# Two graph layers on one core: another order of the setup, bounds kept in half blocks, two buffers for the context products, and an earlier start of layer 1

## The chip, the cores and the metric

The kernel runs on one core of a Trainium2 chip. The metric is the device time of one execution in microseconds (us). Engines are named as in the profile: PE is TensorE (matmuls; PEld are its weight loads), DVE is VectorE, ACT is ScalarE, POOL is GpSimd, SP is the queue that issues most DMAs. POOL and ACT issue some DMAs too. Each engine runs its instructions in the order in which the program gives them.

## The reference

There are 8 batches of 2048 nodes with 256 features, and one adjacency matrix for all of them. Cut to what matters:

```python
def norm(x):      # mean and variance over the features
    return (x - mean(x)) / sqrt(var(x) + 1e-5)

# layer 0: attention in 4 heads of 64, softmax within chunks of 256 keys
h = maximum(norm(x), 0)
q, k, v = h @ Wq.T + bq, h @ Wk.T + bk, h @ Wv.T + bv      # split into heads
s = clip(q @ k_chunk.T / sqrt(64), -10, 10)               # for each of 8 chunks
s = where(adj == 0, -10, s)
ctx = sum over chunks of softmax(s within the chunk) @ v_chunk
out = norm(ctx @ Wo.T + bo + h) * gamma + beta
x = x + out

# layer 1: one head, additive attention over the neighbours
h = maximum(norm(x), 0)
g = h @ W
e = leaky_relu((g @ a1)[:, None] + (g @ a2)[None, :], slope=0.01)
att = softmax(where(adj == 0, -1e9, e))
x = x + maximum(att @ g, 0)
```

All values are float32.

## The kernel before

**Blocks and steps.** The nodes of a batch are cut into four blocks of 512 queries (`nb` 0 to 3) and eight chunks of 256 keys (`j`). Attention has 32 steps of one block and one chunk. A step makes four tiles of logits (`logits`, L490, PE into `ps_s`); `clip` (L530, DVE) clips them from below, and from above by `bounds`, an int8 tile that holds +80 where an edge is and -80 where none is; `exponentials` (L539, ACT); `add` (L545, POOL) halves the work of the sums; `values` (L506, PE into `ps_n`) and `sums` (L518, PE into `ps_t`) multiply with v and with ones; `invert` (L550, ACT) takes the reciprocal; `scale` (L560, DVE) makes the product `prod`, and `gather` (L565) is a DMA on POOL's queue that adds `prod` to the block's `ctxT` in memory. Three steps are in flight at once: `begin(f)` and `end(f)` work on steps f, f-1, f-2 and f-3, in an order written out by hand.

**One order for each engine.** The schedule is manual: what stands first in the program is issued first on its engine. Other work is hung into the steps as pieces: `at(n, ...)` puts a piece at half step n.

**Setup** (L1015 to L1087). For batch 0 the features are normed, turned (L375) and projected to q, k and v (`qk` L434, `values` L448). The adjacency is read in 32 parts of 128 rows by 1024 keys; 24 of them are treated in the setup, 8 inside batch 0's steps. `find` loads rows four parts ahead and calls `missing_of`: DVE compares with zero (L277) into a tile `z`; parts with `half` 0 are read in a permuted order, parts with `half` 1 are read straight and POOL permutes them (L281). `bound` turns z on PE (L292, into `ps_z`) and `keep_bounds` writes the int8 bounds by ACT (L303), into `bounds[0]` or `bounds[1]` on the chip, or else into a small `bound_part`, which a DMA on POOL's queue stores (L306). The bounds of the other blocks are fetched from DRAM (`fetch_bounds`, 1 MB a block, two buffers).

**Between attention and layer 1.** `Between` holds a block's residual, output projection (`output`, L692; `take`, L728), norm, and then the features of layer 1 (`stats1` to `norm1`, turned by `ends(0)`, multiplied with W by `ends(1)`, L814). The blocks are called zero, low, mid and last.

**Layer 1.** `weights` (L940, L946, DVE) makes a piece: the attention weights of four key tiles for one block, masked by `bounds1`; `products` (L963, PE) multiplies a piece with g. There are 16 pieces a batch. In the last batch there is no next batch to hide the passage between the layers; there three first pieces (`early(0)` to `early(2)`) are placed among `last`'s steps:

```python
            last.output(0)
            last.output(1)
            last.take(0)
            last.take(1)
            weights(1)
            mid.ends(0)
            mid.ends(1)
            ...
            accs[0] = one.accumulators(0)
            early(0)
            ...
            early(1)
            last.ends(0)
            last.ends(1)
            early(2)
```

Of the kernel before, what the change touches and what calls it, by code (L numbers as in the profile page):

```python
# [17 lines left out]
P = 128  # L18
# [10 lines left out]
def gnn_two_layers(  # L29
# [139 lines left out]
    def bound_tile():  # L169
        return xpool.tile([P, NT, NB], I8, tag="bound", name="bound", bufs=2)  # L170

    def fetch_bounds(nb):
        t = bound_tile()
        nc.sync.dma_start(t, bound_d[nb])
        return t

    def store_bounds(nb):
        nc.sync.dma_start(bound_d[nb], bounds[nb])
# [88 lines left out]
    def missing_of(rows, t, half):  # L267

        tag = "e" if in_setup[0] else "hn"
        z = work.tile([P, 2 if in_setup[0] else 1, HALF], BF16, tag=tag, name="z", bufs=5)  # L270
        aside = in_setup[0] and half
        apart = dict(t=TB, b=Q)
        if aside:
            src, dst = rows, z[:, 1, :]
        else:
            src, dst = in_blocks(rows), z[:, 0, :].rearrange("p (k t b) -> p k t b", **apart)
        nc.vector.tensor_scalar(  # L277
            dst, src, 0.0, 0.0, op0=ALU.is_equal, op1=ALU.add, accum_out=missing[:, t, half:half + 1],
        )
        if aside:  # L280
            nc.gpsimd.tensor_copy(z[:, 0, :].rearrange("p (k t b) -> p k t b", **apart), in_blocks(z[:, 1, :]))  # L281
        return z[:, 0, :]
# [11 lines left out]

    def keep_bounds(pt, t, half):

        nb, rows, cols = t // TB, slice(half * 8, (half + 1) * 8), slice((t % TB) * P, (t % TB + 1) * P)
        if nb in bounds:
            dst = bounds[nb][:, rows, cols]
# [3 lines left out]
        nc.scalar.activation(dst, pt, AF.Copy, scale=-2.0 * CLIP * SC, bias=CLIP * SC)  # L303
        if nb not in bounds:
            queue = nc.gpsimd if in_setup[0] else nc.scalar
            queue.dma_start(bound_d[nb][:, rows, cols], dst)  # L306
# [162 lines left out]
    class Attention:  # L469
# [55 lines left out]
        def clip(self, n, o):  # L525
            nb, j = self.STEPS[n]
            p, i = self.ORDER[o]
            if (n, p) not in self.e:
                self.e[n, p] = work.tile([P, 2 * KT, NB], F32, tag="e", name="e", bufs=5)
            nc.vector.scalar_tensor_tensor(  # L530
                self.e[n, p][:, i * KT:(i + 1) * KT, :], self.s.pop((n, o)), -CLIP * SC,
                bounds[nb][:, j * KT:(j + 1) * KT, :], op0=ALU.max, op1=ALU.min,
            )
# [19 lines left out]
        def scale(self, n, c):  # L553
# [3 lines left out]
            if j > 0 and c == 0:  # L557
                self.prod[n] = work.tile([P, 2, NB], F32, tag="prod", name="prod", bufs=1)
# [38 lines left out]
        def begin(self, f, pieces=()):  # L597
# [9 lines left out]
            if self.has(f - 1):  # L607
                self.clip(f - 1, 0)
# [270 lines left out]
    class Layer1:  # L879
# [56 lines left out]
        def weights(self, nb, j4):  # L936
            w = work.tile([P, 4, NB], F32, tag="e", name="w", bufs=5)
            for i in range(4):
# [5 lines left out]
                if i % 2:  # L944
                    two = w[:, i - 1:i + 1, :]
                    nc.vector.scalar_tensor_tensor(  # L946
                        two, bounds1[nb][:, j - 1:j + 1, :], 0.0, two, op0=ALU.is_gt, op1=ALU.mult
# [69 lines left out]
    rows = {i: load_rows(*nearest[i]) for i in range(4)}  # L1017
    proj.stats(0, range(TB))
# [4 lines left out]
    turn_weight(raws["v"], wvT)  # L1023
    proj.norm(0, 0)
# [16 lines left out]
    for nb in range(2):  # L1041
        bounds[nb] = bound_tile()
# [4 lines left out]
    for nb in range(NNB - 1):  # L1047
# [28 lines left out]
    att.early(0)  # L1076
    proj.qk(NNB - 1, 0)
# [6 lines left out]
    find(22, 23)  # L1084
    bound(22, 23)
    proj.values(NNB - 1)
    att.early(3)  # L1087
# [5 lines left out]
    def layer1_vector(i):  # L1093
# [12 lines left out]
        2: [lambda: store_bounds(0), lambda: store_bounds(1)],  # L1106
# [11 lines left out]
    for b in range(B):  # L1118
# [19 lines left out]
        def fetch(of, nb):  # L1138
            of[nb] = fetch_bounds(nb)
# [21 lines left out]
        else:  # L1161
            at(6, lambda: fetch(bounds, 1))
        at(PER + 4, lambda: fetch(bounds, 2))
        at(2 * PER + 4, lambda: fetch(bounds, 3))
        at(3 * PER + 4, lambda: fetch(bounds1, 0))
        at(STEPS2 + 2, lambda: fetch(bounds1, 1))
# [106 lines left out]
        else:  # L1273
            one.targets(0, TB)
            one.sources(0)
            mid.stats1(range(TB))
            mid.power1()
            mid.shift1()
            low.ends(1)
            low.sum1()  # L1280
            weights(0)
# [4 lines left out]
            last.output(1)  # L1286
            last.take(0)
            last.take(1)
            weights(1)
# [9 lines left out]
            accs[0] = one.accumulators(0)  # L1299
            early(0)  # L1300
# [6 lines left out]
            weights(2)  # L1307
            last.norm1(0)
# [13 lines left out]
            weights(4)  # L1322

# [3 lines left out]
        for i, (nb, j4) in enumerate(pieces1):  # L1327
            if not ahead and i < 3:
                continue
            if i + 2 < len(pieces1):  # L1330
                weights(i + 2)
            if nb not in accs:
# [12 lines left out]
            if j4 == 0 and nb > 0 and nb + 1 < NNB:  # L1345
                fetch(bounds1, nb + 1)
            if ahead and (nb, j4) == (NNB - 1, 0):
                fetch(bounds, 0)
# [55 lines left out]
```

## Time and profile before

| | us |
|---|---|
| median of 3 runs | 3546.02 (3544.25 to 3546.72) |
| the profiled execution: its own time | 3546.5 |
| its span, first to last instruction | 3544.7 |
| PE busy in the span | 3518.3 (99%) |
| DVE, ACT, POOL busy | 2637.4, 1946.3, 1808.7 |
| mean granted clock of PE | 0.999 |
| loads of bounds, 1 MB each | 62, landing in 6.0 at the median |
| gathers of `prod` into `ctxT` | 224, landing in 4.8 at the median |

Busy time is the union of an engine's instructions. A row of a timeline gives the start, the duration, the engine and line, the operation, what it writes and reads with sizes, how many were merged, and in brackets the idle time of the engine before it with what ended it. A row of waits gives the waiting operation, what it waited for, the total, how often, and the longest. Matmuls follow each other in a pipeline and their ends are modelled, so a PE that is shown busy can still be held up.

### The profile page before, as it was taken

What the parts mean: (1) busy time and instruction counts of PE and PEld (TensorE: products, weight loads), DVE (VectorE), ACT (ScalarE), POOL (GpSimd) and SP (SyncE); (2) the same over time, 40 slices, a digit from 0 to 9 for tenths busy, and PEclk for the clock granted to TensorE, in tenths of its full rate; (3) what the DMA queues carried; (4) which work ended last, traced back from release to release, by engine and by line L of the source; (5) the groups of instructions that cost most, each with busy time, mean ns of one, the idle gap of its engine ahead of it and who ended that gap; (6) DMA issues with size and microseconds to landing.
All of it is one profiled execution on the core that took longest, in us unless ns stands there. A gap on an engine that the chain in (4) does not pass through costs nothing.

```text
span 3544.7 us, 104427 instructions
## 1 busy us (share of the span) xinstructions
PE 3518.3 (99%) x46080; PEld 2185.4 (62%) x46080; DVE 2637.4 (74%) x3979; ACT 1946.3 (55%) x2961; POOL 1808.7 (51%) x1182
## 2 busy tenths in 40 slices
PE   8999999999999999999999999999999999999999
PEld 5455785557755577555875558655586555865568
DVE  7888677876778676786767867678586785857866
ACT  5777326764267632676336762367624676147750
POOL 2678016870178702786027850378404784048841
PEclk9999999999999999999999999999999999999999
DMA  7455423344234442344423444233442334124331
GB/s 235 116 111 124 98 75 86 85 116 86 86 78 91 116 92 71 86 86 121 93 66 86 97 108 93 72 80 91 120 104 55 81 88 122 57 55 91 80 81 42
DMA packets 169111, 329.74 MB, mean 93 GB/s; under 512 B 35664, under 2 KB 97360, under 8 KB 160464
## 3 DMA queue, kind: packets, MB, share of 16 engines
q1 hardware_dynamic: 127696, 203.51, 18.9%
q0 software_dynamic: 32640, 118.50, 18.0%
q8 instruction: 360, 5.90, 0.7%
q10 hardware_dynamic: 8320, 1.05, 0.2%
q14 instruction: 95, 0.78, 0.1%
HBM read 154.14 MB, written 51.43 MB: 58 GB/s over the span
## 4 chain that ended last, share of the span: by engine, by line
PE 97%; DVE 1%; DMA 1%; ACT 0%; issue 0%; POOL 0%; DVEq 0%; POOLq 0%; ACTq 0%
PE ps_s L490 25%; PE ps_n L506 25%; PE ps_s L963 13%; PE ps_t L518 7%; PE ps_n L963 6%; PE ps_t L963 6%; PE ps_t L714 2%; PE ps_t L434 2%; PE ps_n L434 2%; PE ps_s L434 2%; PE ps_t L448 2%; PE ps_n L448 2%; PE ps_t L814 2%; PE ps_n L814 2%; PE ps_n L692 0%; PE ps_t L692 0%
## 5 line engine op out<-in xcount | busy, mean ns | idle before, releaser
L530 DVE SCALAR_TENSOR_TENSOR e<-ps_s,bound 128x1024 f32<-128x1024 f32 x1024 | 1225.1, 1221 | 398.6 <-PE ps_s L490 396.4
L545 POOL TENSOR_TENSOR both<-e 128x1024 f32<-128x1024 f32 x512 | 1219.4, 2406 | 564.2 <-PE ps_t L518 353.5
L490 PE MATMUL ps_s<-q,k 64*32 64x512 f32 x16384 | 1431.7, 590 | 1.6 <-DVE e L530 1.4
L539 ACT ACTIVATE e<-e 128x1024 f32<-128x1024 f32 x1024 | 1050.2, 1050 | 475.6 <-DVE e L530 457.1
L506 PE MATMUL ps_n<-e,v 64*32 64x512 f32 x16384 | 1222.1, 590 | 3.5 <-DVE prod L560 3.5
L506 PEld LDWEIGHTS ps_n<-e,v 64*32 64x32 f32 x16384 | 462.5, 107 | 468.8 <-issue 386.2
L490 PEld LDWEIGHTS ps_s<-q,k 64*32 64x32 f32 x16384 | 460.6, 106 | 447.6 <-issue 332.8
L518 PE MATMUL ps_t<-both,ones 64*32 64x512 f32 x4096 | 536.4, 591 | 0.0
L963 PE MATMUL ps_s<-g,w 128*128 128x257 f32 x2048 | 448.4, 380 | 0.0
L963 PEld LDWEIGHTS ps_s<-g,w 128*128 128x128 f32 x2048 | 388.3, 190 | 56.0
L560 DVE TENSOR_TENSOR prod<-ps_n,rz 128x512 f32<-128x512 f32 x448 | 288.8, 687 | 150.9 <-PE ps_n L506 91.5
L986 POOL TENSOR_TENSOR x<-x,r 128x256 f32<-128x256 f32 x124 | 90.5, 744 | 459.2 <-ACT r L984 458.4
L946 DVE SCALAR_TENSOR_TENSOR w<-bound,w 128x1024 f32<-128x1024 int8 x256 | 314.7, 1229 | 8.7
L354 POOL TENSOR_TENSOR krn<-krn,mv 128x4 f32<-128x4 f32 x28 | 6.8, 242 | 570.6 <-DVE w L940 570.6
L963 PE MATMUL ps_n<-g,w 128*128 128x257 f32 x1024 | 292.4, 382 | 0.0
L963 PE MATMUL ps_t<-g,w 128*128 128x257 f32 x1024 | 289.7, 379 | 0.0
L550 ACT ACTIVATE rz<-ps_t 128x512 f32<-128x512 f32 x256 | 152.6, 596 | 222.5 <-PE ps_t L518 194.7
L940 DVE TENSOR_SCALAR w<-src,cd 128x512 f32<-128x512 f32 x512 | 263.3, 556 | 7.0 <-ACT src L921 6.6
L963 PEld LDWEIGHTS ps_n<-g,w 128*128 128x128 f32 x1024 | 192.8, 190 | 44.4 <-issue 17.6
L565 POOL DMA_DIRECT2D ctxT<-prod x224 | 191.0, 853 | 55.6 <-DVE prod L560 47.9
L963 PEld LDWEIGHTS ps_t<-g,w 128*128 128x128 f32 x1024 | 193.8, 189 | 28.1
L551 ACT ACTIVATE rz<-rz 128x512 f32<-128x512 f32 x256 | 161.4, 630 | 8.1
(137 smaller groups left out, 2908.6 us busy)
## 6 DMA issues: line engine op xcount, KB each, us to landing
ctxT<-prod POOLq DMA_DIRECT2D x224, 512.0 KB, 4.8
bound<-bound_d SPq DMA_DIRECT2D x62, 1024.0 KB, 6.0
turned_d<-squares SPq DMA_DIRECT2D x232, 128.0 KB, 2.4
hT<-turned_d SPq DMA_DIRECT2D x58, 512.0 KB, 4.4
rows<-in_adj_dram SPq DMA_DIRECT2D x32, 512.0 KB, 5.2
x<-in_x_dram SPq DMA_DIRECT2D x32, 512.0 KB, 4.7
out_dram<-x SPq DMA_DIRECT2D x31, 512.0 KB, 2.6
xp<-in_x_dram SPq DMA_DIRECT2D x28, 512.0 KB, 4.1
```

What stands on the lines that cost most here:

```text
L434: nc.tensor.matmul(in_key_order(pp) if i == 0 else pp, w[:, di, do * P:(do + 1) * P], h, start=di == 0, stop=di == FC - 1,)
L490: nc.tensor.matmul(self.s[n, o][c * Q:(c + 1) * Q, kt, :], self.k[p][rows, at:at + Q], self.q[p][rows, nb * NB:(nb + 1) * NB], start=True, ...
L506: made.append(nc.tensor.matmul(self.num[n, c][h * Q:(h + 1) * Q, :], self.v[rows, j * KT + kt, at:at + Q], self.e[n, p][rows, i * KT + kt, :],
L518: nc.tensor.matmul(self.total[n][h * Q:(h + 1) * Q, :], ones[rows, :], self.both[n, h // 2][rows, h % 2, :], start=half == 1, stop=half == 0,)
L530: nc.vector.scalar_tensor_tensor(self.e[n, p][:, i * KT:(i + 1) * KT, :], self.s.pop((n, o)), -CLIP * SC, bounds[nb][:, j * KT:(j + 1) * K ...
L539: nc.scalar.activation(e, e, AF.Exp, scale=1.0 / SC)
L545: nc.gpsimd.tensor_tensor(self.both[n, p], e[:, 0], e[:, 1], op=ALU.add)
L560: nc.vector.tensor_tensor(dst[:, c, :], self.num.pop((n, c)), self.rz[n], op=ALU.mult)
L565: nc.gpsimd.dma_start(self.ctxT[nb], self.prod.pop(n), accum_op=ALU.add)
L940: nc.vector.tensor_scalar(w[:, i, :], self.src[nb], self.cd[:, 0, j:j + 1], self.cd[:, 1, j:j + 1], op0=ALU.mult, op1=ALU.max,)
L946: nc.vector.scalar_tensor_tensor(two, bounds1[nb][:, j - 1:j + 1, :], 0.0, two, op0=ALU.is_gt, op1=ALU.mult)
L963: nc.tensor.matmul(accs[t][:, 0:F + 1], w[:, i, t * P:(t + 1) * P], g[:, j, :], start=j == 0, stop=j == NT - 1,)
```

## The change

It has six parts.

1. Setup: in every part DVE now reads the rows straight and POOL permutes (`aside` holds for both halves). Parts are turned one pair later than before, and q and k of a block stand closer together. `keep_bounds` no longer stores at once; `send_bounds` does, after the next pair of finds. Step 1's first logits and their clip come before the last block's values. 24 transposes of the identity (`warm`) are added at the start.
2. Bounds are kept, stored and fetched in halves of a block (512 KB), with three buffers for two.
3. `prod` has two buffers for one; so have the parts of bounds under two of the tags.
4. Fetches come at regular places: each eighth half step, and each second piece of layer 1.
5. In the last batch, `weights(0)` and `early(0)` come ahead of the last output projection, `weights(1)` ahead of its takes, and mid's stats behind low's end.
6. `clip` of a step's first tile is left out where it was done early.

```diff
     def bound_tile():
-        return xpool.tile([P, NT, NB], I8, tag="bound", name="bound", bufs=2)
-
-    def fetch_bounds(nb):
+        return xpool.tile([P, NT // 2, NB], I8, tag="bound", name="bound", bufs=3)
+
+    def of_half(part):
+        nb, half = part
+        return bound_d[nb][:, half * (NT // 2):(half + 1) * (NT // 2), :]
+
+    def fetch_bounds(part):
         t = bound_tile()
-        nc.sync.dma_start(t, bound_d[nb])
+        nc.sync.dma_start(t, of_half(part))
         return t
...
-        aside = in_setup[0] and half
+        aside = in_setup[0]
...
+    unsent = []
+
+    def send_bounds():
+        while unsent:
+            nb, rows, cols, dst = unsent.pop(0)
+            nc.gpsimd.dma_start(bound_d[nb][:, rows, cols], dst)
+
     def keep_bounds(pt, t, half):
...
-            dst = work.tile([P, 8, P], I8, tag=tag, name="bound_part", bufs=2 if tag == "r" else 1)
+            dst = work.tile([P, 8, P], I8, tag=tag, name="bound_part", bufs=1 if tag == "o4" else 2)
         nc.scalar.activation(dst, pt, AF.Copy, scale=-2.0 * CLIP * SC, bias=CLIP * SC)
-        if nb not in bounds:
-            queue = nc.gpsimd if in_setup[0] else nc.scalar
-            queue.dma_start(bound_d[nb][:, rows, cols], dst)
+        if (nb, half) not in bounds:
+            if in_setup[0]:
+                unsent.append((nb, rows, cols, dst))
+            else:
+                nc.scalar.dma_start(bound_d[nb][:, rows, cols], dst)
...
-                self.prod[n] = work.tile([P, 2, NB], F32, tag="prod", name="prod", bufs=1)
+                self.prod[n] = work.tile([P, 2, NB], F32, tag="prod", name="prod", bufs=2)
...
-            if self.has(f - 1):
+            if (f - 1, 0) in self.s:
                 self.clip(f - 1, 0)
...
+    def warm(times):
+        pt = ps_m()
+        for k in range(times):
+            nc.tensor.transpose(pt[:, k % TB * P:(k % TB + 1) * P], ident, ident)
+
+    warm(16)
     proj.stats(0, range(TB))
     proj.power(0)
     turn_weight(raws["q"], wqT)
     proj.shift(0)
     turn_weight(raws["k"], wkT)
     turn_weight(raws["v"], wvT)
+    warm(8)
...
     def find(*parts):
         for i in parts:
             found[i] = missing_of(rows.pop(i), *nearest[i])
+        send_bounds()
+        for i in parts:
             if i + 4 < len(nearest):
                 rows[i + 4] = load_rows(*nearest[i + 4])
...
-        find(i + 2, i + 3)
-        bound(i, i + 1)
-        proj.qk(nb, 1, ps_h)
-        find(i + 4, i + 5)
-        bound(i + 2, i + 3)
+            find(2, 3)
+            proj.qk(0, 1, ps_h)
+            bound(0, 1)
+        else:
+            bound(i - 2, i - 1)
+            find(i + 2, i + 3)
+            proj.qk(nb, 1, ps_h)
+            bound(i, i + 1)
...
         proj.turn(nb + 1, 1)
+        find(i + 4, i + 5)
...
         proj.values(nb)
+        bound(i + 2, i + 3)
         find(i + 6, i + 7)
-        bound(i + 4, i + 5)
...
     att.early(0)
+    bound(16, 17)
...
     find(22, 23)
+    att.early(3)
+    att.clip(1, 0)
     bound(22, 23)
     proj.values(NNB - 1)
-    att.early(3)
+    send_bounds()
...
+        for k in range(8):
+            at(8 * k + (40 - 24 if b == 0 and k == 3 else 12), lambda k=k: fetch(k + 3))
...
             one.targets(0, TB)
             one.sources(0)
+            weights(0)
+            low.ends(1)
+            low.sum1()
             mid.stats1(range(TB))
             mid.power1()
             mid.shift1()
-            low.ends(1)
-            low.sum1()
-            weights(0)
+            accs[0] = one.accumulators(0)
+            early(0)
             mid.norm1(0)
             mid.norm1(1)
             one.targets(TB, 2 * TB)
             last.output(0)
             last.output(1)
+            weights(1)
             last.take(0)
             last.take(1)
-            weights(1)
...
-            accs[0] = one.accumulators(0)
-            early(0)
...
             weights(2)
+            fetch(11)
...
             weights(4)
+            fetch(12)
...
+            if i % 2 == 0 and (ahead or i < 10):
+                fetch(i // 2 + 11)
```

More of the change, by code (lines that the diff above doesn't have):

```diff
@@ L169, in bound_tile, with store_bounds @@
     def bound_tile():
-        return xpool.tile([P, NT, NB], I8, tag="bound", name="bound", bufs=2)
-    def fetch_bounds(nb):
+        return xpool.tile([P, NT // 2, NB], I8, tag="bound", name="bound", bufs=3)
[3 more added lines that the diff above has]
+    def fetch_bounds(part):
         t = bound_tile()
-        nc.sync.dma_start(t, bound_d[nb])
+        nc.sync.dma_start(t, of_half(part))
         return t
-    def store_bounds(nb):
-        nc.sync.dma_start(bound_d[nb], bounds[nb])
+    def store_bounds(part):
+        nc.sync.dma_start(of_half(part), bounds[part])
     lone = const.tile([P, NT], F32, name="lone")
@@ L293, in turn_missing @@
         return pt
+    unsent = []
[3 more added lines that the diff above has]
+            nc.gpsimd.dma_start(bound_d[nb][:, rows, cols], dst)
     def keep_bounds(pt, t, half):
         nb, rows, cols = t // TB, slice(half * 8, (half + 1) * 8), slice((t % TB) * P, (t % TB + 1) * P)
-        if nb in bounds:
-            dst = bounds[nb][:, rows, cols]
+        if (nb, half) in bounds:
+            dst = bounds[nb, half][:, :, cols]
         else:
             tag = part_tags[(2 * t + half) % 4] if in_setup[0] else "r"
-            dst = work.tile([P, 8, P], I8, tag=tag, name="bound_part", bufs=2 if tag == "r" else 1)
+            dst = work.tile([P, 8, P], I8, tag=tag, name="bound_part", bufs=1 if tag == "o4" else 2)
         nc.scalar.activation(dst, pt, AF.Copy, scale=-2.0 * CLIP * SC, bias=CLIP * SC)
-        if nb not in bounds:
-            queue = nc.gpsimd if in_setup[0] else nc.scalar
-            queue.dma_start(bound_d[nb][:, rows, cols], dst)
+        if (nb, half) not in bounds:
[3 more added lines that the diff above has]
+                nc.scalar.dma_start(bound_d[nb][:, rows, cols], dst)
     def find_lone():
@@ L531, in clip @@
                 self.e[n, p][:, i * KT:(i + 1) * KT, :], self.s.pop((n, o)), -CLIP * SC,
-                bounds[nb][:, j * KT:(j + 1) * KT, :], op0=ALU.max, op1=ALU.min,
+                bounds[nb, j // 4][:, j % 4 * KT:(j % 4 + 1) * KT, :], op0=ALU.max, op1=ALU.min,
             )
@@ L946, in weights @@
                     nc.vector.scalar_tensor_tensor(
-                        two, bounds1[nb][:, j - 1:j + 1, :], 0.0, two, op0=ALU.is_gt, op1=ALU.mult
+                        two, bounds1[nb, j // 8][:, j % 8 - 1:j % 8 + 1, :], 0.0, two, op0=ALU.is_gt, op1=ALU.mult
                     )
@@ L1039, in bound @@
             keep_bounds(turn_missing(found.pop(i)), *nearest[i])
-    for nb in range(2):
-        bounds[nb] = bound_tile()
+    HALVES_OF = [(nb, half) for nb in range(NNB) for half in range(2)]
+    for part in HALVES_OF[:3]:
+        bounds[part] = bound_tile()
     proj.stats(1, range(TB))
@@ L1105, in gnn_two_layers @@
         1: [lambda: raws.update(o=load_output_weight(wo)), layer1_weight],
-        2: [lambda: store_bounds(0), lambda: store_bounds(1)],
+        2: [lambda: [store_bounds(part) for part in HALVES_OF[:3]]],
         5: [pe(lambda: turn_weight(raws["o"], woT))],
@@ L1136, in early, with fetch @@
             one.products(accs[0], ws.pop(i), i)
-        def fetch(of, nb):
-            of[nb] = fetch_bounds(nb)
+        def fetch(k):
+            of = bounds if k < 8 or k >= 16 else bounds1
+            of[HALVES_OF[k % 8]] = fetch_bounds(HALVES_OF[k % 8])
         for nb in range(NNB - 1):
@@ L1160, in gnn_two_layers @@
                 at(n + 7, lambda nb=nb: ahead.send(nb))
[L1161 to L1166, printed above, removed]
+        for k in range(8):
+            at(8 * k + (40 - 24 if b == 0 and k == 3 else 12), lambda k=k: fetch(k + 3))
         at(STEPS2 - 6, last.load)
@@ L1344, in gnn_two_layers @@
                 one.finish(nb - 1, accs[nb - 1])
[L1345 to L1348, printed above, removed]
             if j4 == 1 and nb > 0:
```

## The prediction

> **What bounds the kernel now.** I read the page first, then TensorE's waits, then the timeline round the longest of them.
>
> ```profile
> PE 3518.3 (99%) x46080; PEld 2185.4 (62%) x46080; DVE 2637.4 (74%) x3979; ACT 1946.3 (55%) x2961; POOL 1808.7 (51%) x1182
> ```
>
> TensorE is busy all the time, so only its idle time, and matmuls whose records are stretched by a wait or a slow clock, can be won. TensorE's waits:
>
> ```profile
> PE ps_z L292 <- POOL z L281: 6.8, 4, 4.3
> PE ps_n L250 <- DMA raw<-in_L_gnn_Wq_dram: 5.5, 1, 5.5
> PE ps_n L506 <- DVE prod L560: 3.5, 4, 1.4
> PE ps_n L692 <- DVE sd L823: 3.1, 1, 3.1
> PE ps_s L490 <- DVE e L530: 1.4, 1, 1.4
> ```
>
> Columns: us in total, times, longest. Three places: the setup (L292, L250, L490), the context products (L506), the last output projection (L692). The setup's longest wait in the timelines of TensorE and of GpSimd:
>
> ```profile
> 70.25 1.65 PE L292 MATMUL ps_z<-ident_b,z 128*128 128x128 bf16 x24
> 76.24 1.03 PE L292 MATMUL ps_z<-ident_b,z 128*128 128x128 bf16 x8 [4.33 <-POOL z L281]
> 77.07 3.73 PE L448 MATMUL ps_t<-wvT,hT 128*128 128x256 f32 x8
> ```
>
> ```profile
> 73.30 1.80 POOL L306 DMA_DIRECT2D bound_d<-bound_part  x2 [0.95 <-ACT bound_part L303]
> 75.09 1.09 POOL L281 COPY z<-z 128x1024 bf16<-128x1024 bf16 x1
> ```
>
> The last copy of z stood behind two stores of bounds, which waited for ScalarE. After the 4.33 us gap the eight projections took 3.73 us against 1.99 for the same eight at 24.48: the clock had halved. The waits of VectorE, and two batches out of the table by stretches (length, then PE):
>
> ```profile
> DVE prod L560 <- DMA ctxT<-prod: 38.9, 53, 2.7
> ```
>
> ```profile
> 1726.39:2160.24 433.85, 433.85 (x5722) 270.88 (x5721) 322.84 (x489) 239.02 (x365) 223.56 (x145) 1.00 0.38 91
> 2594.24:3033.76 439.52, 437.62 (x5722) 269.74 (x5721) 322.30 (x489) 239.49 (x365) 223.68 (x145) 1.00 0.35 89
> ```
>
> The same work took 5.67 us longer in one batch, mostly not shown as idle: TensorE's waits understate the third row. The tail:
>
> ```profile
> 3410.38 1.03 PE L814 MATMUL ps_t<-w1s,hT 128*128 128x258 f32 x4
> 3414.47 1.99 PE L692 MATMUL ps_n<-woT,ctxT 128*128 128x256 f32 x8 [3.05 <-DVE sd L823]
> 3423.14 14.04 PE L963 MATMUL ps_s<-g,w 128*128 128x257 f32 x64
> 3437.01 0.60 PE L375 MATMUL ps_n<-ident,hn 128*128 128x128 f32 x4
> ```
>
> Two layer-1 pieces (64 matmuls) fill the time until the last block's features are ready to turn (L375): that chain ends at 3437.1 (ScalarE's norm), just when TensorE comes for it. It has no slack.
>
> **What the Trainium skill says.** *TensorE: Matmul & The Clock Gate*, "What's actually happening": an idle window of about 3.4 us halves the matmul clock until a busy window has passed; the trace agrees (above; PEclk 0.74 over 70 to 80 us). *Perfetto Trace Analysis*, "Optimization Strategy": the same gap repeating can mean too few buffers; L560's 53 waits on one buffer agree. *DMA: Bandwidth & Descriptors*, "Anatomy of one DMA": a DMA's semaphore wait is done by the issuing sequencer; the queue at 73.30 agrees. *SBUF — State Buffer*, "Who interferes with whom": some VectorE operations and GpSimd block each other for a whole instruction; L940 takes 544 ns alone and up to 1054 beside GpSimd's adds.
>
> **The change, part by part.**
>
> *Context products (L558), two buffers.* A product waits until the gather of the step before has landed. Step by step in the timeline, waits of 0.65, 1.12, 1.52 and 2.35 us lengthened their step (7.72 us when undisturbed) by 0.13, 0.65, 1.12 and 1.82: 0.5 us is slack, the rest reaches TensorE whole. 38.9 - 53 x 0.52 = 11.3; the wait at 2804.7, put down to L490, is the gather issued at 2797.76, late by its landing at 2804.6, and adds 2.2 - 0.5 = 1.7. Sum **-13**. The gather itself lands in 4.8 us at the median and 9.0 at worst, against a step of 7.72, so GpSimd's next one hardly waits for it. Check from below: the five longer batches exceed the shortest by 1.13, 1.69, 0.66, 0.15 and 5.67, 9.3 in six batches of eight. Bounds -8 and -15.
>
> *Setup.* All 24 finds now read straight (1.22 us, not 1.99) and GpSimd does 12 more copies of 1.11 us: VectorE saves 12 x 0.77 = 9.2, GpSimd gains 13.3 and four more sends of 0.89, and stays under 40 us of some 70. Per block of the setup VectorE then needs 12.2 us (six finds 7.2, stats and shift 2.4, v 1.3, copy 0.6, waits 0.7) against TensorE's 14.2; before it needed 14.5 and paced the setup. The 24 warming transposes take 0.22 us each at the low clock (L250: four in 0.87): sixteen, 3.5 us, from the identity's end at 1.44 lie under the 5.46 us wait for the weights; eight, 0.9 to 1.75, before the first norm at 8.55; at worst they cost 0.8. What they bring is the clock for q(0): 3.65, not 4.66. By hand, on the old clock time: q(0) 11.3 to 15.0; k(0), held by ScalarE's read of q, to 18.6; z0, z1 (found by 16.8, copied by 17.9) to 19.5, where the same work ended at 23.5; turn to 20.4; v(0), behind ScalarE's read of z0, 20.8 to 24.4; z2, z3 25.3; q(1) 28.8; z4, z5 29.7. k(1) starts at 29.7 instead of 33.93: -4.2. Later, 0.3 of small waits, the 4.33 and the slow clock's 2.6 (L448 2.2, L292 0.4) go; the first logits of step 1 and their clip, moved ahead of the last values, cover the 1.42. In all -12.9. Loads of rows are now issued after a pair of finds, not after each, so up to 1.2 us later; VectorE's 2 us to spare per block take that. New waits take some back: part 22's bounds go into the buffer of part 18, whose send now stands behind the copies of parts 22 and 23: issued 67.8, landed (5.7) 73.5; ScalarE's read and the exponential queued behind it end at 76.4, and TensorE wants that at 74.4: +2. Six sends and an add on GpSimd end 1 us after TensorE asks for the sum: +1. **-9.5**, bounds -13 and -5: the rows, x and bounds then need 3.9 MB in 14.2 us, 275 GB/s, where the densest stretch moved 302.
>
> *Bounds in halves.* 125 loads of 512 KB replace 62 of 1 MB, three half buffers two whole ones. In attention a half serves four steps (31 us) and is fetched seven steps ahead; in layer 1 it serves two pieces (13.9 us) and is fetched some four pieces (27.8 us) ahead; before, two pieces ahead. A 512 KB load lands in about 4.7 us (row of x). The 63 more issues at 0.4 us sit on SP, which mostly waits. Stores of the first three halves replace two whole ones. **0**, bounds -1 and +3; lost cover is a rival.
>
> *Tail.* The first layer-1 piece (6.94 us) goes ahead of L692: its weights, 4.35 us of VectorE from 3408.5, are half done when TensorE is free at 3411.25. The 3.05 goes. What else is moved is small: mid's four stats (2.2 us of VectorE), power and shift go behind low's values; two fetches on SP go ahead of the last sends and wait for weights that are made before those anyway. But the projection then starts at 3418.2 or later, not 3414.47, and with it the chain to L375, 22.5 us long, which before ran beside 22 us of work (two pieces among it) and now beside 15. L375 comes at least 3.7 later. Also the second piece's weights now stand ahead of the take of the projection, and they need targets that ScalarE makes after mid's norm: with 1 to 2 us of blocking by GpSimd's adds, mid's values wait another 1 to 2. TensorE then idles some 5.5 us after the one piece, over a clock window: 1.5 more (half of the 2.6 above for its chance). **+6**, bounds 0 and +9.
>
> Sum: -13 - 9.5 + 0 + 6 = **-16.5**. The profiled run took 3546.5 (span 3544.7, 1.8 around it), 0.5 above the median 3546.02: 3530.0, taken as **3530** for the median too.
>
> **Rivals.** *The tail costs nothing:* if VectorE's chain shortens because its small copies come earlier, the tail brings 3 instead: -13 - 9.5 - 3 = -25.5, 3520. Against it: the chain had no slack. *A wait in place of the one removed:* GpSimd waits at its queue for the earlier gather, with both adds behind it, and TensorE for the sums; -9.5 + 6 = -3.5, 3542. For it: GpSimd is in order; against: a step has 2.2 us of GpSimd to spare (4.7 adds, 0.8 issue). The setup giving nothing (transfers bound it) with the rest as forecast gives -7, 3539. *Slower:* the halves come late. Three halves hold less ahead than two wholes, and SP takes its DMAs in order, behind stores that wait up to 32.7 us for GpSimd's adds. With 125 loads, a mean wait of 16.5 / 125 = 0.13 us at the clip or mask eats the whole gain, and 0.35 makes +44 - 16.5: 3573. Against it: the distances above.
>
> **How the numbers follow.** Forecast 0.60 (its own range 3522 to 3538), tail free 0.21, wait moved or setup empty 0.13, halves late 0.06. Range 3517 to 3542 leaves out the late halves and little else. No change means within 0.2% (7 us), about what a measurement of this kernel can tell. Faster 0.81, same 0.13, slower 0.06.
>
> **What would show it.** Right: no L560 waits on ctxT<-prod, batches all near 433.9; k(1) four us earlier, no gap of 4 us at L292 and PEclk 1.00 to 100 us; L692 without a wait, and a new gap of 4 to 7 us before the last block's L375. Wrong: GpSimd waiting for gathers; VectorE's L530 or L946 waiting for bound; a L375 in the tail at 3437 or before on the same scale.

## The result, and the profile after

| | before | changed |
|---|---|---|
| median, us | 3546.72 (3544.25 to 3549.36, 7 runs) | 3535.36 (3534.5 to 3537.41, 7 runs) |
| profiled execution, us | 3546.5 (span 3544.7) | 3534.5 (span 3532.7) |

The ratio is 0.9968, 95% interval 0.9956 to 0.9979: 11.4 us less. The forecast was 3530, in a range of 3517 to 3542: right in sign, and 5 us too hopeful. Most lines move by 13: L560 is L573 after the change, L506 is L519, L692 is L705, L963 is L976, L375 is L388, L940 and L946 are L953 and L959.

The summary and TensorE's waits (in total, times, longest):

```profile
PE 3512.5 (99%) x46104; PEld 2370.3 (67%) x46104; DVE 2632.9 (75%) x3979; ACT 1945.8 (55%) x2961; POOL 1825.8 (52%) x1198
```

```profile
PE ps_s L976 <- DVE w L959: 5.0, 1, 5.0
PE ps_n L388 <- ACT hn L379: 4.6, 1, 4.6
PE ps_n L1034 <- POOL ident masks.py:199: 1.5, 1, 1.5
PE ps_n L519 <- DVE prod L573: 1.4, 1, 1.4
PE ps_n L519 <- ACT bound_part L314: 0.8, 1, 0.8
```

All of the old list is gone: GpSimd's z (6.8), the products (3.5, but for one of 1.4 at the end), the wait ahead of the projection (3.1). Two new waits stand at the top, and both are in the last passage. The same two batches as in the prediction, the fourth and the sixth of its table, cut somewhat later (from one batch's first sums to the next one's: length, then PE; the kernel before, cut in the same way, has 433.86 and 439.52):

```profile
1826.19:2259.63 433.44, 433.44 (x5732) 307.01 (x5724) 322.60 (x489) 239.00 (x366) 223.65 (x145) 1.00 0.38 91
2692.98:3126.37 433.39, 433.39 (x5732) 296.93 (x5724) 311.58 (x449) 228.27 (x338) 223.15 (x141) 1.00 0.34 81
```

The stretch that had been 439.52 us is 433.39, as long as the other. VectorE's list has no wait of L573 for ctxT<-prod. GpSimd's list has one row of waits for gathers, 1.9 us in all, so the wait did not move there:

```profile
POOL both L558 <- DMA ctxT<-prod: 1.9, 3, 0.9
```

The setup, from TensorE's timeline:

```profile
28.84 3.65 PE L447 MATMUL ps_s<-hT,wkT 128*128 128x512 f32 x8
...
76.02 2.45 PE L519 MATMUL ps_n<-e,v 64*32 64x512 f32 x26 [0.77 <-ACT bound_part L314]
...
82.92 1.92 PE L519 MATMUL ps_n<-e,v 64*32 64x512 f32 x32
```

k(1) starts 5.1 us earlier. The last row, the first values of step 1, stood at 92.98 before: the setup's end came 10.1 us earlier. This row is the mark for the setup's end in what follows. The last passage:

```profile
3387.86 1.03 PE L827 MATMUL ps_t<-w1s,hT 128*128 128x258 f32 x4
3393.85 8.74 PE L976 MATMUL ps_s<-g,w 128*128 128x257 f32 x32 [4.96 <-DVE w L959]
3402.43 1.89 PE L705 MATMUL ps_n<-woT,ctxT 128*128 128x256 f32 x8
...
3410.99 7.10 PE L976 MATMUL ps_s<-g,w 128*128 128x257 f32 x32
3422.71 1.95 PE L388 MATMUL ps_n<-ident,hn 128*128 128x128 f32 x4 [4.61 <-ACT hn L379]
...
3437.07 1.03 PE L903 MATMUL ps_n<-w1s,hsum 128*128 128x256 f32 x4
```

The first row, low's last values, comes 22.5 us earlier than before (3410.38). From here the kernel loses: 4.96 us of waiting for the first weights in place of 3.05 ahead of the projection, products at a slow clock (8.74 us, not 7.10), then a gap of 4.61 and four transposes in 1.95 us in place of 0.60. The account of the two profiled runs, by rows that both have: the setup -10.1; the batches after it -12.4 (22.5 - 10.1); the last passage, from the start of low's last values to the start of the product for the mean (L903, the last row; before it was L890, at 3449.07), 38.7 before and 49.2 now, +10.5. Sum -12.0, and the two executions differ by 12.0.

Why the first weights were late is in VectorE's timeline, read beside GpSimd's:

```profile
3386.11 6.43 DVE L953 TENSOR_SCALAR w<-src,cd 128x512 f32<-128x512 f32 x2 [0.43 <-ACT src L934]
3392.57 1.22 DVE L959 SCALAR_TENSOR_TENSOR w<-bound,w 128x1024 f32<-128x1024 int8 x1
3393.72 1.00 DVE L953 TENSOR_SCALAR w<-src,cd 128x512 f32<-128x512 f32 x2
```

```profile
3385.98 0.86 POOL L578 DMA_DIRECT2D ctxT<-prod  x1 [5.60 <-DVE prod L573]
3386.58 1.56 POOL L776 TENSOR_TENSOR x<-x,o 128x512 f32<-128x512 f32 x1
3387.81 1.55 POOL L772 TENSOR_TENSOR x<-x,beta_r 128x512 f32<-128x512 f32 x1
3389.03 1.54 POOL L748 TENSOR_TENSOR hn<-hn,bo_r 128x512 f32<-128x512 f32 x1
3390.26 1.53 POOL L772 TENSOR_TENSOR x<-x,beta_r 128x512 f32<-128x512 f32 x1
```

Two L953 take 6.43 us, and the next two, with GpSimd quiet, 1.00. GpSimd's four additions follow each other without a gap from 3386.58 to 3391.79. In narrower windows of VectorE's timeline the first two L953 stand apart:

```profile
3386.11 5.97 DVE L953 TENSOR_SCALAR w<-src,cd 128x512 f32<-128x512 f32 x1 [0.43 <-ACT src L934]
3392.00 0.54 DVE L953 TENSOR_SCALAR w<-src,cd 128x512 f32<-128x512 f32 x1
```

It is the first that was held, and it ended 0.3 us after the last addition. It started 0.5 us before the first of them, while GpSimd still issued the last gather; whether that issue holds VectorE too is not shown. That the additions hold it is so far a reading; no_train tests it.

### The profile page after: what moved, and what is told of

The parts are those of the page before. It is cut to its first block, busy times and chain, and to the rows that moved or that the text cites. A ratio compares the mean times of both kernels' runs of the same rounds, so it can differ in the third digit from the quotient of the medians.

```text
span 3532.7 us, 104631 instructions
## 1 busy us (share of the span) xinstructions
PE 3512.5 (99%) x46104; PEld 2370.3 (67%) x46104; DVE 2632.9 (75%) x3979; ACT 1945.8 (55%) x2961; POOL 1825.8 (52%) x1198
## 4 chain that ended last, share of the span: by engine, by line
PE 98%; DVE 1%; ACT 1%; DMA 0%; issue 0%; POOL 0%; ACTq 0%; DVEq 0%; POOLq 0%
PE ps_s L503 25%; PE ps_n L519 25%; PE ps_s L976 12%; PE ps_t L531 7%; PE ps_n L976 6%; PE ps_t L976 6%; PE ps_t L727 2%; PE ps_t L447 2%; PE ps_n L447 2%; PE ps_s L447 2%; PE ps_n L827 2%; PE ps_t L827 2%; PE ps_n L461 1%; PE ps_t L461 1%; PE ps_t L705 0%; PE ps_n L705 0%
## 5 line engine op out<-in xcount | busy, mean ns | idle before, releaser
L503 PE MATMUL ps_s<-q,k 64*32 64x512 f32 x16384 | 1328.4, 590 | 0.1
L519 PE MATMUL ps_n<-e,v 64*32 64x512 f32 x16384 | 1114.6, 589 | 2.1 <-DVE prod L573 1.4
L503 PEld LDWEIGHTS ps_s<-q,k 64*32 64x32 f32 x16384 | 524.0, 106 | 386.5 <-issue 248.7
L519 PEld LDWEIGHTS ps_n<-e,v 64*32 64x32 f32 x16384 | 556.9, 107 | 332.0 <-issue 200.0
L531 PE MATMUL ps_t<-both,ones 64*32 64x512 f32 x4096 | 553.2, 590 | 0.0
L976 PE MATMUL ps_s<-g,w 128*128 128x257 f32 x2048 | 450.2, 381 | 5.0 <-DVE w L959 5.0
L976 PEld LDWEIGHTS ps_s<-g,w 128*128 128x128 f32 x2048 | 389.4, 190 | 61.8 <-DVE w L959 5.4
L573 DVE TENSOR_TENSOR prod<-ps_n,rz 128x512 f32<-128x512 f32 x448 | 288.9, 687 | 133.4 <-ACT rz L564 70.9
L959 DVE SCALAR_TENSOR_TENSOR w<-bound,w 128x1024 f32<-128x1024 int8 x256 | 314.7, 1229 | 8.7
L976 PE MATMUL ps_n<-g,w 128*128 128x257 f32 x1024 | 292.4, 382 | 0.0
L976 PE MATMUL ps_t<-g,w 128*128 128x257 f32 x1024 | 289.8, 380 | 0.0
L953 DVE TENSOR_SCALAR w<-src,cd 128x512 f32<-128x512 f32 x512 | 268.7, 567 | 9.9 <-ACT src L934 7.0
L531 PEld LDWEIGHTS ps_t<-both,ones 64*32 64x32 f32 x4096 | 156.3, 105 | 100.5 <-SPq L475 43.8
L976 PEld LDWEIGHTS ps_n<-g,w 128*128 128x128 f32 x1024 | 192.8, 190 | 44.3 <-issue 17.6
L976 PEld LDWEIGHTS ps_t<-g,w 128*128 128x128 f32 x1024 | 193.8, 189 | 28.2
```

Of the source, the lines that this page charges most:

```text
L503: nc.tensor.matmul(self.s[n, o][c * Q:(c + 1) * Q, kt, :], self.k[p][rows, at:at + Q], self.q[p][rows, nb * NB:(nb + 1) * NB], start=True, ...
L519: made.append(nc.tensor.matmul(self.num[n, c][h * Q:(h + 1) * Q, :], self.v[rows, j * KT + kt, at:at + Q], self.e[n, p][rows, i * KT + kt, :],
L531: nc.tensor.matmul(self.total[n][h * Q:(h + 1) * Q, :], ones[rows, :], self.both[n, h // 2][rows, h % 2, :], start=half == 1, stop=half == 0,)
L573: nc.vector.tensor_tensor(dst[:, c, :], self.num.pop((n, c)), self.rz[n], op=ALU.mult)
L953: nc.vector.tensor_scalar(w[:, i, :], self.src[nb], self.cd[:, 0, j:j + 1], self.cd[:, 1, j:j + 1], op0=ALU.mult, op1=ALU.max,)
L959: nc.vector.scalar_tensor_tensor(two, bounds1[nb, j // 8][:, j % 8 - 1:j % 8 + 1, :], 0.0, two, op0=ALU.is_gt, op1=ALU.mult)
```

## The experiments

Where nothing else is said, each is the changed kernel with one edit, timed in rounds with the kernel before. That kernel's median was 3552.25 in the first group of four, 3548.56 and 3548.51 in the other two; so differences of 2 or 3 us between medians of different groups are not told from none, and the traces decide there. The changed kernel itself was not timed again. In each group one run whose trace comes out as good as equal to its own can stand in for it: w1_behind (3535.78) beside one_prod, no_train and old_tail; no_warm (3536.35) beside old_setup, half_aside and new_tail; half_aside_tags (3534.78) beside old_order, halves_alone and old_tail_tags. Differences below are from the changed kernel's 3535.36.

**one_prod.**

```diff
-            dst = work.tile([P, 8, P], I8, tag=tag, name="bound_part", bufs=1 if tag == "o4" else 2)
+            dst = work.tile([P, 8, P], I8, tag=tag, name="bound_part", bufs=2 if tag == "r" else 1)
...
-                self.prod[n] = work.tile([P, 2, NB], F32, tag="prod", name="prod", bufs=2)
+                self.prod[n] = work.tile([P, 2, NB], F32, tag="prod", name="prod", bufs=1)
```

> The changed kernel with one buffer for prod in place of two (the parts of bounds that share its tag have one, too); everything else stays. Theory: the second buffer took away the waits of the products L573 for the gather, 11 us of the gain (steps of 7.73 us in batches 1 to 7 again summing to about 13 to 18 us over the undisturbed length a batch, where the changed kernel has 12.3), so about 3545.5 us in the profiled run, 3534.5 + 11, with some 50 waits of L573 on ctxT<-prod of 35 to 40 us in all. Rival: the steps became even because the bounds come in halves at regular places, and the 1 MB loads had slowed the gathers; then the waits with one buffer are fewer and shorter than before, 3536 to 3539.

Measured: 3547.22, 11.9 us more than with two buffers (11.4 more than w1_behind); ratio to before 0.999 (0.9981 to 0.9999). VectorE's list has the old wait again:

```profile
DVE prod L573 <- DMA ctxT<-prod: 41.2, 50, 2.2
```

The first theory holds; regular fetches in halves did not shorten it. In the trace the loss lies in the batches: from the mark of the setup's end to low's last values they take 3316.1 us, 3304.9 in the changed kernel. The second buffer is worth 11 to 12 us.

**halves_alone.** The kernel before with the bounds in halves and the regular fetches (cut):

```diff
-        return xpool.tile([P, NT, NB], I8, tag="bound", name="bound", bufs=2)
+        return xpool.tile([P, NT // 2, NB], I8, tag="bound", name="bound", bufs=3)
...
-        at(PER + 4, lambda: fetch(bounds, 2))
+        for k in range(8):
+            at(8 * k + (40 - 24 if b == 0 and k == 3 else 12), lambda k=k: fetch(k + 3))
```

> The kernel before with the bounds in half blocks, three buffers and the regular fetches, and nothing else of the change (old setup, one buffer for prod, old order of the last passage). Theory: the halves cost and bring nothing (0, bounds -1 and +3): the time of before, the steps of the batches as uneven as before, no wait of the clip or the mask for bound. Rival: the regular halves alone made the gathers quicker; then 3 to 6 us less than before.

Measured: 3548.36 against 3548.51, ratio 1.000 (0.9991 to 1.0008). The products' waits stayed (45.7 us, 51 times), and neither the clip nor the mask waited for bounds. The halves cost nothing and bring nothing by themselves.

**old_setup.** The setup of before: its order, half of the parts read permuted, bounds sent at once, no transposes (cut):

```diff
-    warm(16)
...
-        aside = in_setup[0]
+        aside = in_setup[0] and half
...
-            bound(i - 2, i - 1)
-            find(i + 2, i + 3)
-            proj.qk(nb, 1, ps_h)
-            bound(i, i + 1)
+        find(i + 2, i + 3)
+        bound(i, i + 1)
+        proj.qk(nb, 1, ps_h)
```

> The changed kernel with the setup of before: its order, VectorE reading half of the parts permuted, bounds sent at once, no warming transposes; bounds stay in halves (three of the first four halves are kept, where before four were). Theory: the new setup gave 10 us, and they go: 3544 to 3545, k(1) near 33.9 us and a wait of some 4 us of ps_z for GpSimd's z again. Rival: the first attention steps hide part of a late setup; then 3539 to 3541.

Measured: 3545.72, 10.4 more (9.4 more than no_warm), and the long wait is back in TensorE's timeline:

```profile
77.50 1.03 PE L296 MATMUL ps_z<-ident_b,z 128*128 128x128 bf16 x8 [4.33 <-POOL z L285]
78.33 2.94 PE L459 MATMUL ps_t<-wvT,hT 128*128 128x256 f32 x8
```

The attention steps hide nothing of a late setup. Which of its edits gave the 10 us, the next four runs tell.

**old_order.** As old_setup, but with `aside = in_setup[0]` kept: VectorE reads every part straight.

> The changed kernel with the setup order of before (bounds sent at once, no warming transposes), but every part read straight by VectorE and permuted by GpSimd. Theory of the prediction: VectorE's reading paced the old setup (14.6 us a block), and without its 9.2 us the blocks take 14.2 and most of the gain stays: 3536 to 3539. Rival: the order gave the gain, since a part is now turned a pair later than it is found; with the old order GpSimd's twelve more copies stand right ahead of the turns, TensorE's waits of ps_z for z get longer than the 6.8 us of before, and the time is 3543 to 3548.

Measured: 3544.36, 9.0 more than the changed kernel. The rival is right. In the timeline the blocks did get quicker (k of two following blocks 14.2 us apart, 14.6 in old_setup), as the prediction said of VectorE's pace; but then TensorE stood 4.93 us for one z:

```profile
74.23 2.07 PE L296 MATMUL ps_z<-ident_b,z 128*128 128x128 bf16 x16 [4.93 <-POOL z L285]
```

GpSimd's timeline of the same stretch shows what was ahead of that copy: a sum of attention and two stores of bounds, which wait for ScalarE.

```profile
67.68 2.37 POOL L556 TENSOR_TENSOR both<-e 128x1024 f32<-128x1024 f32 x1
71.28 1.80 POOL L317 DMA_DIRECT2D bound_d<-bound_part  x2 [1.24 <-ACT bound_part L314]
73.08 2.12 POOL L285 COPY z<-z 128x1024 bf16<-128x1024 bf16 x2
```

**half_aside.** The new order, but VectorE reads the parts of half 0 permuted:

```diff
-        aside = in_setup[0]
+        aside = in_setup[0] and half
```

> The changed kernel with its new setup order, but VectorE reading the parts of half 0 permuted itself (1.99 us, not 1.22) and GpSimd copying only the parts of half 1. Theory of the prediction: VectorE paced the setup, 14.5 us a block against TensorE's 14.2, so its 9.2 us come back as 3 to 6: 3537.5 to 3540.5. Rival: the order gave the gain (parts turned a pair later, sends behind the next finds), and VectorE's reading costs nothing: 3534 to 3535.5.

Measured: 3538.13 (3536.08 to 3542.21), 2.8 more: the first theory by its number, though by the medians alone it is not told from none (1.8 more than no_warm). The profiled run, 3542.21, is the slowest of the seven, so its trace shows the loss at its largest. Its blocks are 14.2 us apart, as in the changed kernel, so VectorE did not pace them. The first logits come 6.7 us later than in the changed kernel, and 5.8 of this comes at one place, in ScalarE's and TensorE's timelines:

```profile
53.53 1.02 ACT L314 ACTIVATE bound_part<-ps_z 128x1024 int8<-128x1024 bf16 x1 [4.27 <-DMA bound_d<-bound_part]
```

```profile
54.61 3.78 PE L461 MATMUL ps_n<-wvT,hT 128*128 128x256 f32 x8 [3.30 <-ACT bound_part L314]
```

Part 13's bounds wait on ScalarE until those of part 9 have left the one buffer that they share (tag o4), and part 9's send stood in GpSimd's queue behind copies that waited for VectorE. The clock halved after it (3.78 us, not 1.99).

**half_aside_tags.** The same, with five buffers in turn:

```diff
-    part_tags = ["r", "o4", "r", "prod"]
+    part_tags = ["r", "prod", "o4", "r", "prod"]
+    stored = [0]
...
-            tag = part_tags[(2 * t + half) % 4] if in_setup[0] else "r"
+            tag = part_tags[stored[0] % 5] if in_setup[0] else "r"
+            stored[0] += 1
```

> The run half_aside (VectorE reads the parts of half 0 permuted, new order) with one edit more: the stored parts of bounds take the five buffers r, prod, o4, r, prod in turn, where before parts 9, 13, 17 and 21 shared the one o4. Theory: VectorE's longer reading cost its 3 us only by way of GpSimd's queue: the send of part 9 stood behind copies that waited for VectorE, and part 13's bounds waited for that send on ScalarE (4.27 us), then TensorE (3.3 us) for ScalarE. With other buffers both waits go: 3534 to 3535.5. Rival: VectorE's pace itself is felt; then 3537 to 3539 as in half_aside.

Measured: 3534.78, and in its timeline TensorE has no wait of over 0.4 us between q(1) and the first step. So in the new order the reading of VectorE is free; what it had cost came through one buffer and one queue. The mark that stands at 82.92 in the changed kernel stands at 93.02 in old_setup, 91.00 in old_order and 83.44 here. One trace is not exact to better than a microsecond: five other runs with the changed setup have it between 81.8 and 82.6, and halves_alone, with the setup of before, at 91.66. So straight reading alone brings 0.7 to 2.0 of the 10 us, the order alone (with enough buffers) 8.2 to 9.6.

**no_warm.** Without `warm(16)` and `warm(8)`.

> The changed kernel without the 24 warming transposes. Theory: only q(0) gets slower, 4.7 us for 3.7, and the rest of the setup follows it: 1 us more, 3535.5. Rivals: everything up to the next wait runs at half clock for another window, 3 us more, 3537.5; or ScalarE's and VectorE's chain to q(0) and k(0) hides the clock, 3534.5.

Measured: 3536.35, by the median not told from the changed kernel; in the timeline the mark stands at 82.48, within the 81.8 to 82.9 of the runs with the same setup and the transposes. q(0) had the full clock:

```profile
11.01 3.70 PE L447 MATMUL ps_s<-hT,wqT 128*128 128x512 f32 x8 [0.35 <-DVE hT L421]
```

In half_aside_tags, with all 24 transposes, q(0) took 5.40 us. Warming did not decide it; of the three forecasts the second rival, no loss, is the nearest, for another reason than it gives.

**no_train.** The last block's three additions leave GpSimd:

```diff
-        at(STEPS2 + 3 + late, lambda: last.bias(1))
-        at(STEPS2 + 4, lambda: last.beta(0))
-        at(STEPS2 + 5, lambda: last.beta(1))
+        if ahead: ...
...
             weights(0)
             low.ends(1)
             low.sum1()
+            last.bias(1)
+            last.beta(0)
+            last.beta(1)
```

> The changed kernel with three of the last block's additions in the last batch (bias(1), beta(0), beta(1)) made by VectorE behind the first piece's weights and no longer by GpSimd ahead of them. Theory: GpSimd's row of four additions without a pause held VectorE's second L953 for its whole length, 5.2 us. Then the two L953 take 2 to 2.6 us in place of 6.4 (one addition of GpSimd is left), TensorE waits 1.0 to 1.8 for w at L976 in place of 4.96 and keeps its clock there (6.9 to 7.1 us for the 32 products, not 8.7): 5 to 6 us less, 3529. VectorE's additional 2.1 us lie beside those products. Rival: L953 was long for another reason (its cd or src came late): the wait stays at 5, and the time at 3534 to 3537.

Measured: 3530.79, 4.6 less. With one addition of GpSimd left, in VectorE's and TensorE's timelines:

```profile
3385.96 2.78 DVE L953 TENSOR_SCALAR w<-src,cd 128x512 f32<-128x512 f32 x2 [0.43 <-ACT src L934]
```

```profile
3390.05 7.21 PE L976 MATMUL ps_s<-g,w 128*128 128x257 f32 x32 [1.31 <-DVE w L959]
...
3404.96 1.14 PE L827 MATMUL ps_n<-w1s,hT 128*128 128x258 f32 x4 [0.88 <-DVE o L741]
...
3418.46 1.95 PE L388 MATMUL ps_n<-ident,hn 128*128 128x128 f32 x4 [4.54 <-ACT hn L379]
```

The wait shrank by 3.65, as much as three additions last at their spacing of 1.23 us, and the first L953 alone takes 2.32 in place of 5.97. The products ran at full clock. The reading holds: GpSimd's row of additions held VectorE. With the projection earlier, mid's values now wait 0.88 us for the take (L741), which stands behind the second piece's weights. The gap at L388 is as long as it was, 4.54, with its slow clock: the other half of the loss, which old_tail takes back.

**w1_behind.**

```diff
-            weights(1)
             last.take(0)
             last.take(1)
+            weights(1)
```

> The changed kernel with the second piece's weights behind the takes of the last output projection, as before the change, and nothing else moved. Theory: with the projection as late as it is now, the weights ahead of the takes are nearly hidden (they end 0.1 us after the projection), and behind the takes their 4.35 us stand in the chain to the last block's L388: the gap there grows from 4.6 to some 8 to 9 us, and the run takes 3537 to 3539. Rival, as in the prediction: the weights ahead of the takes delay mid's values by 1 to 2 us, and the run gets 1 to 2 us faster, 3533.

Measured: 3535.78: neither theory, no difference. VectorE's timeline shows why:

```profile
3407.12 0.99 DVE L953 TENSOR_SCALAR w<-src,cd 128x512 f32<-128x512 f32 x2
...
3411.97 0.16 DVE L836 COPY sd<-ps_t 128x2 f32<-128x2 f32 x1 [0.22 <-ACT g L835]
3412.05 0.42 DVE L356 BATCH_NORM_STATS2 stats<-o 128x6 f32<-128x256 f32 x1
```

In program order the last block's stats stand behind mid's four copies of sd, and these wait for mid's values whether the weights are ahead of the take or behind it. The weights lie in that wait.

**old_tail.** The order of before, as quoted at the top: `weights(0)` behind mid's stats, the takes, `weights(1)`, and `early(0)` behind `last.scaled`.

> The changed kernel with the order of before for the passage between the layers of the last batch: the first piece's weights behind mid's stats, its products behind the last projections, the second piece's weights behind the takes. Theory: the new order cost 10.5 us (from the last L827 of low to the mean at L903, 50.1 us against 39.6), and all of it comes back: 3524.0 in the profiled run, the wait ahead of L705 near 3.05 again, no gap at the last block's L388. Rival: part of that tail comes from the bounds in halves and their later fetches, which stay; then 3527 to 3530.

Measured: 3525.58, 9.8 less than the changed kernel; ratio to before 0.9927 (0.9912 to 0.9942). The rows of the passage:

```profile
3392.14 3.78 PE L705 MATMUL ps_n<-woT,ctxT 128*128 128x256 f32 x8 [3.05 <-DVE sd L836]
3395.71 3.20 PE L705 MATMUL ps_t<-woT,ctxT 128*128 128x256 f32 x8
...
3403.86 14.04 PE L976 MATMUL ps_s<-g,w 128*128 128x257 f32 x64
3417.74 0.60 PE L388 MATMUL ps_n<-ident,hn 128*128 128x128 f32 x4
```

The 3.05 wait is back, no gap stands ahead of L388. From low's last values to the mean the passage takes 41.7 us, start to start; 3.1 of these are a slow clock in the projection (6.8 us for its 16 matmuls, 3.7 in the kernel before), and without them it is as long as before, 38.7.

GpSimd's four additions stood there before the change too, from 3409.10 to 3414.31. VectorE's timeline beside them, in the kernel before:

```profile
3408.12 0.42 DVE L343 BATCH_NORM_STATS2 stats<-x 128x6 f32<-128x256 f32 x1
...
3410.70 0.43 DVE L343 BATCH_NORM_STATS2 stats<-x 128x6 f32<-128x256 f32 x1 [1.42 <-POOL x L763]
...
3412.71 1.63 DVE L354 TENSOR_TENSOR rn<-rn,mv 128x4 f32<-128x4 f32 x1 [0.84 <-ACT rn L350]
```

The stats beside the additions took no longer than elsewhere, but one had to wait 1.42 us for the result of an addition, and a small product that takes 0.16 us elsewhere took 1.63. The copies of sd for which the projection waits stood behind both. So the old 3.05 comes in part from the same row of additions, and the change moved the stats, which the additions do not stretch, away from them and the weights, which they hold, beside them. No run joins the old order with additions that have left GpSimd; what that would bring is not shown.

**new_tail.** Half a piece ahead of the projection, stats ahead of mid's copies, weights in halves, the additions on VectorE (cut):

```diff
-            weights(0)
+            one.half_weights(w0, 0, 0, 0)
...
-            early(0)
+            one.products(accs[0], w0, 0, (0, 1))
...
+            last.stats(range(TB))
             mid.ends(0)
-            mid.ends(1)
-            last.stats(range(TB))
...
+            one.products(accs[0], w0, 0, (2, 3))
...
-            early(1)
+            one.products(accs[0], w1, 1, (0, 1))
             last.ends(0)
             last.ends(1)
+            one.products(accs[0], w1, 1, (2, 3))
```

> The changed kernel with a third order for the last passage: only the first half of the first piece (16 products, 3.5 us) ahead of the last output projection, the other half behind mid's values; the last block's stats ahead of mid's copies of sd; the second piece's weights in halves in the gaps that VectorE has while ScalarE makes rn; and the three additions bias(1), beta(0), beta(1) on VectorE. Theory: the passage is bound by the start of the last projection (not before its gather lands, some 1.7 us after TensorE has nothing else) and by the chain from there to the last block's L388, 22.5 us before and 20.3 now; that chain held 4.5 us of waiting for mid's values, and gets 18 to 19 us long. The half piece starts 1.0 us after low's values, the projection 5 us after their last start plus 0 to 1, no gap of over 0.7 us at L388, and from the last L827 of low to L903 37 to 38.5 us, where the changed kernel has 50.1 and the order of before 39.6: 3522 in a run with full clock. Rival: the chain keeps its length, since ScalarE's share sets it; then L388 waits 3 to 4 us, with half the clock behind it, and the time is 3525 to 3528.

Measured: 3525.70. TensorE's timeline:

```profile
3389.84 3.74 PE L998 MATMUL ps_s<-g,w 128*128 128x257 f32 x16 [1.31 <-DVE w L983]
3393.41 1.89 PE L705 MATMUL ps_n<-woT,ctxT 128*128 128x256 f32 x8
...
3410.80 0.33 PE L388 MATMUL ps_n<-ident,hn 128*128 128x128 f32 x1 [1.33 <-ACT hn L379]
...
3413.39 2.09 PE L827 MATMUL ps_n<-w1s,hT 128*128 128x258 f32 x4 [0.26 <-ACT hT L799]
```

The chain from the projection to L388 did shrink, to 17.4 us: the theory's mechanism, and more than it asked. But the half piece that went ahead is missing later, and TensorE again waits at L388 and then runs slowly. The time is the rival's, 3525 to 3528, though the chain did not keep its length. Here, too, the work moved ahead of the projection only moved the idle time.

**old_tail_tags.** old_tail with the five buffers of half_aside_tags.

> The run old_tail (the change with the old order of the last passage) with the five buffers for the stored parts in turn, as in half_aside_tags. Theory: the waits of bound_part for bound_d on ScalarE (4.3 to 5.4 us) go, and with them what TensorE sees of them, 0.2 at L461 and 0.8 to 1.4 at L519: 0.5 to 1.5 us less than old_tail, 3524.5. Rival: other waits take their place (the send of part 18 still stands behind two copies): 3525.6.

Measured: 3524.49 (3522.71 to 3525.25), ratio to before 0.9929 (0.9916 to 0.9942). ScalarE's three waits for buffers, 4.3 us in all, became one of 4.3, that of part 23, which now takes the buffer of part 18; TensorE sees 0.6 of it, where old_tail's list has none. So the rival is right as to the waits, and the 1.1 us between the medians is within the spread. It, old_tail and new_tail are the fastest here, not told apart by their medians, and all three beat the changed kernel clearly.

## Why the prediction was right, and where not

The parts, undone one at a time, against those forecast:

| part | forecast | bounds | measured |
|---|---|---|---|
| two buffers for the products | -13 | -15, -8 | -11.9 (one_prod) |
| setup | -9.5 | -13, -5 | -10.4 (old_setup) |
| bounds in halves | 0 | -1, +3 | -0.2 (halves_alone, against before) |
| last passage | +6 | 0, +9 | +9.8 (old_tail) |
| sum | -16.5 | | -12.7, and the whole -11.4 |

**Products: right.** The sum over the waits less half a microsecond each was within 10% by the medians (11.9), and the traces say 11.1. The rival in which the wait moves to GpSimd is excluded by its list (1.9 us in all).

**Setup: right in size, in part wrong in its reason.** The prediction says that VectorE "paced the setup", 14.5 us a block against TensorE's 14.2. That pace was there (14.6 against 14.2), but straight reading alone brings only 0.7 to 2.0 us. The sum by hand is better than that sentence: most of it are waits that go (4.2 us up to k(1), measured 5.1; then the 4.33 with the slow clock behind it, and the 1.42), and the runs show that they go with the order, since a part is turned a pair later and GpSimd's sends stand behind finds. The new wait for a buffer of bounds, forecast with +2, came with 0.8 at L519; a wait for the sums, forecast with +1, is not in the list. The terms as given, -12.9, +2 and +1, make -9.9 and not -9.5. Warming, forecast to bring q(0) at 3.65 us, decided nothing.

**Bounds: right.** The rival with late halves did not come.

**Last passage: the failed term, beyond its upper bound.** "The 3.05 goes" was wrong: a wait of 4.96 took its place, ahead of L976, so that the sign "L692 without a wait" came true all the same. The prediction counted the first weights as 4.35 us of VectorE and put GpSimd's additions there at nothing; only at the second piece did it allow "1 to 2 us" for them. The first L953 was held for 5.4 us, a little longer than the whole row of four lasts (5.2). The prediction saw the longest single one (1054 ns beside additions) and did not ask how many additions follow each other without a gap. The Trainium skill, *SBUF — State Buffer*, "Who interferes with whom", says that VectorE in some of its modes, which `tensor_scalar` can enter, and GpSimd block each other for a whole instruction; here the block lasted over four instructions. The projection was to start 3.7 later than before in the passage and started 10.5 later: 5.0 of waiting and 1.8 of slow clock more than the 3.7, of which no_train takes back all but 1.6.

Smaller terms partly cancel. The second piece's weights ahead of the takes were to delay mid's values by 1 to 2 us: w1_behind shows 0 where the projection is late, and no_train 0.88 where it is earlier. The chain to L375 was called without slack; measured, it takes 20.3 us where it had 22.5. About 1.4 of this was slack: before, ScalarE's four rows of half a microsecond began at 3435.06, so that L375 could have begun with the first of them at 3435.6, and TensorE came at 3437.01. The other 0.9 is that the last block's stats came earlier after the projection's start (9.3 us, not 10.2). The gap ahead of L388 was 4.6; the prediction names 5.5, though its own chain of 22.5 us beside 15 of work leaves over 7. The slow clock after the gap was taken at 1.5 for its chance; it cost 2.3.

The whole stayed within the range because the error sits in one term, 4 us of 16. That the products came 1 to 2 us short and the setup up to 1 us over, so that the two nearly cancel, is luck.

## What to carry to other kernels

Before work is put ahead of a late stage, look at what the engine that prepares it shares: a row of GpSimd's additions without a gap held one VectorE instruction for its whole length here, and the instruction then shows as one long row; what the additions do not stretch, here the stats, is the better company for them. Where a chain through several engines set the end of a stage, work for TensorE moved ahead of it only moved the idle time to its end; shorten the chain, or leave the filler beside it. And where an experiment undoes an edit and loses what theory says, look at the place of the loss before the theory is believed: half_aside's median fitted the theory, and its trace shows one shared buffer.

## What was not expected of the hardware

A wait of 3.05 us ahead of the projection halved TensorE's clock in some executions and not in others: the projection's 16 matmuls took 3.7 us in the kernel before, 5.3 to 6.8 in old_tail, old_tail_tags and halves_alone. The Trainium skill, *TensorE: Matmul & The Clock Gate*, "What's actually happening", gives about 3.4 us as the idle window after which the clock is halved, and says that the window runs free, so that the moment of a change of clock varies. The waits shown here are shorter than that and still cost clock, so an idle window need not have been all empty; no run separates this from a wait that is longer than the profile shows. In new_tail, too, the stretch was not empty: eight transposes stood between the end of L998 at 3409.5 and L827 at 3413.4, and the next matmuls were still slow (2.09 us, not 1.28).
